# First image behind attention: constants in three packed loads, later expert weights, half a norm beside half a net, tap sums through GpSimd

## Chip, core and metric

The kernel runs on one core of a Trainium2 chip. The metric is the device time of one execution in microseconds (us). A profile shows one execution on that core; its times count from the first instruction of that execution. The engines are called PE (TensorE; PEld are its weight loads), DVE (VectorE), ACT (ScalarE), POOL (GpSimd) and SP (SyncE, which here only issues loads and stores). ACT and POOL issue loads as well; the profile writes ACTq and SPq for that part of an engine.

## What is computed

Four images of 384 channels and 32 x 32 pixels go through two layers, all in fp32:

```python
# layer 0
x = x + attention(ln_c(x))      # 8 heads, relative tables for q, k and v, then out @ w_proj + b_proj
t = tokens(x)
t = t + ffn(ln_t(t))            # weights are kron products: 384 -> 1536 (gelu) -> 384
# layer 1
x = x + conv(ln_c(x))           # depthwise: 7x7 + 5x3 + 3x5 + (1x7 then 7x1) + (1x5 then 5x1) + biases
t = tokens(x)
t = t + moe(ln_t(t))            # 4 experts, 2 per token, 384 -> 1536 (gelu) -> 384, weighed by the gates
```

ln_c and ln_t both normalise one pixel over its 384 channels.

## The kernel before, in words

The work goes in three phases. qkv_phase computes queries, keys and values and writes them to DRAM. attention_phase runs over the eight heads, and within a head over the 32 image rows; its order is written out by hand and pinned. rest_phase does everything else, image by image. Within rest_phase a scheduler orders what isn't pinned, by the dependences of the operations, and the generators that are stepped side by side decide what it may mix.

Channels lie on the 128 partitions in three chunks (KC = 3), pixels along the free side. An image of 1024 pixels is worked in two halves of 512 (TOK).

**End of attention** (L628 to L637). The last head's second half of rows is finished behind the loop: the values are multiplied (values), the reciprocal sums go to DRAM (keep, rd), four table products are added to the result o (value_table, add_table), and for each of the two groups of images a spread of the reciprocals is loaded (spread, tile rb, one buffer) and multiplied into o on POOL (normalise, L490). The result is stored to ao_d by two transfers that POOL issues (store, L494). The first half of the rows was stored before, by SP.

**Constants** (const, L906). 24 arrays are loaded into a tile each, by 24 transfers on ACT's queue. w_proj and b_proj belong to the projection, fold, c_fc and c_proj to the net, w77 to b35 to the convolution, gate_w to slot0 to the gates and to the lists of slots. A transfer has one of eight completion counters, given out in turn to the transfers of SP and ACT together; one that is given a counter waits until the transfer that had it before has landed.

**Image 0, front** (front, L926). For each half the attention's result (tile at) and x (into xb) are loaded by SP; then both halves are projected (L948), added to x (L951) and their statistics taken (token_stats, L65: PE transposes a block of 128 pixels into row_ps, DVE takes mean and variance); then the net runs over one half after the other (L958 to L1000): u_ps is the folded input, f_ps the hidden layer, which ACT turns by Gelu into hs, o_ps gathers it, and ffn_ps spreads it back to the channels, to be added to xb (L997). fold is scaled and centred before (L1375 to L1377); its sum_ps matmuls stand in PE's line between the first matmul of the projection and the others.

**Behind front.** preload(wts[0]) (L1380) loads two blocks of expert weights of 2.5 MB each by SP. POOL clears img, the padded image (L1381). combined (conv_weights, L705) adds the small convolutions into the 7 x 7 weights, on DVE.

**Image 0, convolution** (first, L1326). normalise (L1004) takes statistics of both halves, and writes (x - mean) to xc and the factors to scale_sb; image (L1018) multiplies them into img. Then the 49 taps are shared: DVE does channel chunk 0 and four rows of chunk 1 by multiply-adds (convolve, L1038), PE does the rest in four parts (taps_by_matmul, L1058): for each part 98 matmuls with diagonal weights (made by POOL, L1064, two products of 3136 elements each) into two banks, which ACT copies (L1092); two matmuls add the copies into a third bank (taps_ps, a single buffer, L1093), and DVE adds that to xb (L1096). gates (L1129) need the whole of xb; gate_ps (L647) is their first matmul.

**After that** the front, norm and convolution of images 1 to 3 run beside the experts' blocks (blocks, L1189 on; e_ps and y_ps are theirs), with a planner that steps a list of others() by costs (more, L1402).

Of the kernel before, what the change touches and what calls it, by code (L numbers as in the profile page):

```python
# [11 lines left out]
F32 = mybir.dt.float32  # L12
AF = mybir.ActivationFunctionType
ALU = mybir.AluOpType
# [4 lines left out]
P = 128  # L19
B, C, IMG = 4, 384, 32  # L20
N = IMG * IMG
# [22 lines left out]
HS = 5  # L44
# [8 lines left out]
NOT_LAST = (2 * (B - 1) * N + NEXP * (BLK - 1)) // BLK - sum(COUNTS[:-1])  # L53
MAXB = B * N // BLK
OUTSIDE = 1e6


def bcast(ap, dim, n):
# [133 lines left out]
def attention_phase(tc, cst, held, tabs, tv, qk_d, v_d, ao_d, heads):  # L192
# [31 lines left out]
    with ExitStack() as es:  # L224
# [252 lines left out]
            dst = o.rearrange("p g (y x) -> p g y x", x=IMG)[: 64 + HD, :, :, XT * g : XT * (g + 1)]  # L477
            nc.gpsimd.tensor_tensor(dst, dst, tvs, ALU.add)

        def spread(rd, g):  # L480
            rb = work.tile([P, YT * IMG], F32, tag="rb", name="rb", bufs=1)
            for r in range(2):
                dma(
                    rb[64 * r : 64 * r + 64],
                    bass.AP(rd.tensor, rd.offset + (2 * g + r) * N, [[0, 64], [1, YT * IMG]]),
                )
            return rb

        def normalise(o, g, rb):
            nc.gpsimd.tensor_tensor(o[:, g], o[:, g], rb, ALU.mult)  # L490

        def store(h, o, y, issue=dma):
            for r in range(2):
# [29 lines left out]
        for n, h in enumerate(heads):  # L523
# [104 lines left out]
            if not last:  # L628
                batch = (h, o, IMG - 1, keep(rT))
                blk = nblk  # L630
        values(o, IMG - 1)
        rd = keep(rT)
        for g in range(IMG // XT):
            add_table(o, g, value_table(g))
        for g in range(2):
            normalise(o, g, spread(rd, g))
        store(heads[-1], o, IMG - 1, nc.gpsimd.dma_start)  # L637


def gate_logits(nc, pools, ident, gw, x, logits):  # L640
# [64 lines left out]
def conv_weights(nc, const, pool):  # L705

    w7, bias = const("w77", [P, KC, 7, 7]), const("b77", [P, KC])
    small = [(const(name, [P, KC, kh, kw]), kh, kw) for name, kh, kw in (("w53", 5, 3), ("w35", 3, 5))]
    lines = [(const(f"w{n}w", [P, KC, 1, n]), const(f"w{n}h", [P, KC, n, 1]), n) for n in (7, 5)]
    biases = [const(name, [P, KC]) for name in ("b53", "b35")]  # L710
    yield w7, bias
    for t, kh, kw in small:
        y, x = (7 - kh) // 2, (7 - kw) // 2
        for k in range(KC):
            dst = w7[:, k, y : y + kh, x : x + kw]
            nc.vector.tensor_tensor(dst, dst, t[:, k], ALU.add)
    for tw, th, n in lines:
        full = pool.tile([P, KC, n, n], F32, name=f"cw_f{n}")
        o = (7 - n) // 2
        for k in range(KC):  # L720
            nc.vector.tensor_tensor(full[:, k], bcast(tw[:, k], 1, n), bcast(th[:, k], 2, n), ALU.mult)
            dst = w7[:, k, o : o + n, o : o + n]
            nc.vector.tensor_tensor(dst, dst, full[:, k], ALU.add)
    for t in biases:
        nc.vector.tensor_tensor(bias, bias, t, ALU.add)


def slot_positions(nc, pools, cst, image, count, total):
# [151 lines left out]
def rest_phase(tc, cst, x, ao_d, ins, xs_d, y_d, x2_d, out):  # L880
# [9 lines left out]
    with ExitStack() as es:  # L890
# [8 lines left out]
        ps_y = es.enter_context(tc.tile_pool(name="r_ps_y", bufs=1, space=PSUM))  # L899
        stp = (small, ps_h, "h")  # L900

        def after(ins_, other):
            sync = mybir.DependencyInfo(mybir.DependencyClass.Sync, mybir.DependencyReason.DATA)
            tc.add_manual_dep(ins_.ins, other.ins.name, sync, reason="slots are written in pieces")

        def const(name, shape):  # L906
            t = wp.tile(shape, F32, name=f"c_{name}")
            nc.scalar.dma_start(t, ins[name])
            return t

        wproj = const("w_proj", [P, KC, C])
# [11 lines left out]
        pc["one"], pc["slot0"] = one, const("slot0", [P, NEXP])  # L923
        img = wp.tile([P, KC, IMG + 6, IMG + 6], F32, name="img")

        def front(b, xb):  # L926

            banks = [(ps_h, "h", None)] * 3 + ([(ps_y, "y", 2)] * 2 + [(ps_y, "t", None)] if b <= 1 else [])  # L930
            halves = [xb[:, :, half * TOK : (half + 1) * TOK] for half in range(2)]
            ats = []
            for half, xs in enumerate(halves):
                at = work.tile([P, KC, TOK], F32, tag="xc", name="at")
                nc.sync.dma_start(at, ao_d[half][:, b].rearrange("(k p) n -> p k n", p=P))
                nc.sync.dma_start(
                    xs, x[b, :, half * TOK : (half + 1) * TOK].rearrange("(k p) n -> p k n", p=P)
                )
                ats.append(at)
                yield 0.0, 0.0  # L940
            for _ in range(3):
                yield 0.0, 0.0
            scales = []
            for at, xs in zip(ats, halves):
                for m in range(KC):
                    ps = ps_h.tile([P, TOK], F32, tag="h", name="proj_ps")
                    for k in range(KC):
                        nc.tensor.matmul(  # L948
                            ps, wproj[:, k, m * P : (m + 1) * P], at[:, k, :], start=(k == 0), stop=(k == KC - 1)
                        )  # L950
                    nc.vector.scalar_tensor_tensor(  # L951
                        xs[:, m, :], ps, bproj[:, m : m + 1], xs[:, m, :], ALU.add, ALU.add
                    )
                    yield 0.7, 2.7

                _, rstd = yield from token_stats(nc, stp, ident, xs, cst["eps5"])
                scales.append(rstd)
            for rstd, xs in zip(scales, halves):  # L958
                scale = to_partitions(nc, (small, ps_m, "m"), ident, one, rstd)
                scale_sb = work.tile([P, TOK], F32, tag="scale", name="scale")  # L960
                nc.scalar.copy(scale_sb, scale)


                ps = ps_m.tile([P, TOK], F32, tag="m", name="u_ps")
                for k in range(KC):
                    nc.tensor.matmul(ps, fold[:, k, :], xs[:, k, :], start=(k == 0), stop=(k == KC - 1))
                u = small.tile([P, TOK], F32, tag="u", name="u")
                nc.vector.tensor_tensor(u, ps, scale_sb, ALU.mult)
                yield 1.4, 3.5

                po = ps_m.tile([P, TOK], F32, tag="m", name="o32_ps")
                pend = []
                for f0 in range(0, NF + 3, 3):
                    phs = []
                    for f in range(f0, min(f0 + 3, NF)):
                        pool, tag, bufs = banks[f % len(banks)]
                        ph = pool.tile([P, TOK], F32, tag=tag, name="f_ps", **({"bufs": bufs} if bufs else {}))
                        lo = f % 4 * 32
                        nc.tensor.matmul(ph, c1t[lo : lo + 32, f // 4, :], u[lo : lo + 32, :], start=True, stop=True)
                        phs.append((f, ph))  # L980
                    for f, hs in pend:
                        lo = f % 4 * 32
                        nc.tensor.matmul(
                            po[lo : lo + 32, :], cp1t[:, f, :], hs, start=(f < 4), stop=(f >= NF - 4)
                        )
                    pend = []
                    for f, ph in phs:
                        hs = hid.tile([P, TOK], F32, tag="hs", name="hs", bufs=HS)
                        nc.scalar.activation(hs, ph, AF.Gelu)  # L989
                        pend.append((f, hs))  # L990
                    yield 0.0, 2.2
                o32 = small.tile([P, TOK], F32, tag="u", name="o32")
                nc.scalar.copy(o32, po)
                for m in range(KC):
                    ps = ps_h.tile([P, TOK], F32, tag="h", name="ffn_ps")
                    nc.tensor.matmul(ps, spread[:, m * P : (m + 1) * P], o32, start=True, stop=True)
                    nc.vector.scalar_tensor_tensor(  # L997
                        xs[:, m, :], ps, cp2[:, m : m + 1], xs[:, m, :], ALU.mult, ALU.add
                    )
                yield 2.1, 2.7  # L1000

        pause = wp.tile([P, 1], F32, name="pause")

        def normalise(xb, halves):  # L1004

            for half in range(2):
                xs = xb[:, :, half * TOK : (half + 1) * TOK]
                mean, rstd = yield from token_stats(nc, stp, ident, xs, cst["eps6"])
                mps = to_partitions(nc, (small, ps_m, "m"), ident, one, mean)
# [39 lines left out]

        wts = [[wp.tile([P, WROW], F32, name=f"w{i}{fh}") for fh in range(2)] for i in range(2)]  # L1050

        def preload(w):
            for fh in range(2):
                nc.sync.dma_start(w[fh], ins["w12"][fh * P : (fh + 1) * P, :])

        none = wp.tile([P, 2, 1], F32, name="none")
        nc.vector.memset(none, 0.0)
        def taps_by_matmul(xb, parts):  # L1058
# [15 lines left out]
            for k, y0, ny in parts:  # L1074
# [18 lines left out]
                    nc.tensor.matmul(po[64 * h : 64 * h + 64, :n], half, e[:, :n], start=True, stop=True)  # L1093
                yield
                acc = xb[:, k, y0 * IMG : y0 * IMG + n]
                nc.vector.tensor_tensor(acc, acc, po[:, :n], ALU.add)  # L1096
                yield

        def new(shape, name, dt=F32):
# [223 lines left out]
            yield from gates(b)  # L1323
            yield from scatter(b, pause)

        def first():  # L1326


            half, own = IMG // 2, 4
# [2 lines left out]
                xbs[0], [(2, 0, half), (2, half, half), (1, own, rest), (1, own + rest, rest)]  # L1332
            )
            next(taps)
            halves = []
            yield from normalise(xbs[0], halves)
            yield from image(halves)
            for _ in convolve(0, xbs[0], [(0, 0, IMG), (1, 0, own)]):
                for _ in range(3):
# [35 lines left out]
        for k in range(KC):  # L1375
            nc.vector.tensor_scalar_mul(fold[:, k, :], fold[:, k, :], cf2[:, k : k + 1])
        center(nc, ps_m, "m", one, fold)  # L1377
        for _ in enter(0):
            pass
        preload(wts[0])  # L1380
        nc.gpsimd.memset(img, 0.0)  # L1381
        for _ in combined:
            pass
        center(nc, ps_m, "m", one, gw)
        reached = set()
        todo = others()
        for i, _ in enumerate(first()):
            if 6 <= i < 8:
                next(todo)
        for i, _ in enumerate(dispatch(0)):  # L1390
# [128 lines left out]
```

## Time and profile before

| what | value |
|---|---|
| median of 9 runs | 3103.27 us |
| lowest, highest | 3094.65, 3106.81 us |
| the profiled execution's own time | 3101.2 us |
| its span, first to last instruction | 3099.4 us |
| mean granted clock of PE | 0.976 |
| busy over the span: PE, DVE, ACT, POOL | 2927.0, 1928.6, 1378.7, 1165.6 us |
| last product of attention on PE ends | 1500.1 us |
| convolution of image 0 on DVE starts | 1603.4 us |
| gate_ps of image 0 starts | 1701.0 us |

How to read it. A line of a timeline has the start, the busy time, the engine, the line of the kernel, the operation, output<-input, shape, how many, and in brackets how long the engine sat idle before it and what ended that. A line of the waits has who waited for whom, the us in total, the times, and the longest. A line of the chain has the start, the duration and the step; the chain is followed back from the last instruction of the execution to what released each step. Idle time of an engine that nothing waits for costs nothing.

### The profile page before, as it was taken

The page shows a single profiled execution, that of the slowest core. Times are in us where ns is not written, and L with a number is a line of the kernel's source. Part 1 is how long each engine was busy: PE and PEld are TensorE (multiplying, and loading weights), DVE is VectorE, ACT ScalarE, POOL GpSimd, SP SyncE. Part 2 cuts the span into 40 slices and gives each one's busy share as a digit, 9 for nine tenths or more (in the row PEclk, how much of TensorE's full clock was granted, in tenths as well). Part 3 has the DMA queues.
Part 4 walks back from the last instruction along what each step waited for, and adds up shares of the span by engine and source line. Part 5 has one row for each costly group of instructions (what it writes and reads, how often), then busy time and mean ns, then how long its engine had stood idle before and what let it go on. Part 6 is the DMA issues. An engine that isn't in the chain of part 4 may idle for free.

```text
span 3099.4 us, 63826 instructions
## 1 busy us (share of the span) xinstructions
PE 2927.0 (94%) x25591; PEld 2031.5 (66%) x25591; DVE 1928.6 (62%) x3595; ACT 1378.7 (44%) x2839; POOL 1165.6 (38%) x1115
## 2 busy tenths in 40 slices
PE   8997999999999999999698989998999999999996
PEld 4544676767777777677433455664677777778775
DVE  2226787878787878787466699998999610001101
ACT  1105666666666666666220513333342423333332
POOL 3224737474747473737200321131234322114422
PEclk9998999999999999999899999999999999999998
DMA  3796566656565656564401331530444144375852
GB/s 126 261 317 207 134 199 138 200 139 199 139 199 139 199 139 199 134 203 117 164 21 57 126 124 75 219 146 16 171 174 179 41 175 176 143 288 197 310 193 73
DMA packets 265720, 500.56 MB, mean 162 GB/s; under 512 B 137248, under 2 KB 190112, under 8 KB 257744
## 3 DMA queue, kind: packets, MB, share of 16 engines
q1 hardware_dynamic: 168944, 246.73, 25.7%
q0 software_dynamic: 43552, 228.24, 19.9%
q10 hardware_dynamic: 52928, 21.53, 3.6%
q8 instruction: 201, 3.29, 0.5%
q14 instruction: 95, 0.78, 0.1%
HBM read 543.58 MB, written 152.37 MB: 225 GB/s over the span
## 4 chain that ended last, share of the span: by engine, by line
PE 69%; DVE 12%; issue 10%; DMA 3%; POOL 3%; ACT 2%; ACTq 0%; SPq 0%; POOLq 0%; DVEq 0%
PE e_ps L1243 15%; PE y_ps L1221 14%; PE t_ps L397 8%; DVE xb L1038 7%; PE av_ps L214 7%; PE sc_ps L214 7%; PE tabq_ps L214 5%; PE a_ps L407 3%; PE tv_ps L214 2%; PE tabk_ps L214 2%; DVE extra L389 1%; DVE oT L466 1%; PE row_ps L74 1%; PE qk_ps L162 1%; DMA qk_d<-qk_sb 1%
## 5 line engine op out<-in xcount | busy, mean ns | idle before, releaser
L1243 PEld LDWEIGHTS e_ps<-xT,w 128*128 128x128 f32 x4824 | 654.7, 193 | 229.7 <-ACT hs L989 16.1
L340 POOL TENSOR_TENSOR bias<-b,s 128x416 f32<-128x416 f32 (+24 forms) x656 | 659.6, 1044 | 171.5 <-DMA s<-sd 155.1
L1243 PE MATMUL e_ps<-xT,w 128*128 128x128 f32 x4824 | 673.2, 277 | 19.7 <-DVE xb L951 8.0
L1221 PE MATMUL y_ps<-w,eh 128*128 128x384 f32 x1608 | 650.9, 489 | 6.1 <-ACT eh L1246 6.1
L1246 ACT ACTIVATE eh<-e_ps,w 128x128 f32<-128x128 f32 x804 | 294.1, 368 | 740.3 <-PE e_ps L1243 728.8
L1038 DVE SCALAR_TENSOR_TENSOR xb<-img,c_w,xb 128x1024 f32<-128x1024 f32 (+1 forms) x539 | 611.3, 1199 | 0.0
L1211 POOL DMA_INDIRECT w<-in_w,row x134 | 163.1, 1217 | 773.0 <-PE y_ps L1221 265.7
L389 DVE TENSOR_REDUCE extra<-arow 128x32 f32<-128x32 f32 (+24 forms) x768 | 381.3, 555 | 9.9 <-ACT arow L378 5.8
L368 DVE CUSTOM_DVE_ANT_0 arow<-sc_ps,bias 128x1024 f32<-128x1024 f32 x256 | 312.6, 1221 | 95.4 <-issue 52.6
L397 PEld LDWEIGHTS t_ps<-ident,arow 128*128 128x128 f32 x2048 | 220.5, 142 | 173.0 <-ACT aT L398 100.6
L378 ACT ACTIVATE arow<-arow,nm 128x1024 f32<-128x1024 f32 x256 | 302.9, 1183 | 65.0 <-DVE nm L368 64.9
L398 ACT COPY aT<-t_ps 128x512 f32<-128x512 f32 x512 | 278.9, 604 | 93.2 <-PE t_ps L397 92.9
L1224 DVE TENSOR_TENSOR yo<-y_ps,w 128x384 f32<-128x384 f32 x67 | 37.3, 557 | 443.4 <-PE y_ps L1221 443.4
L397 PE MATMUL t_ps<-ident,arow 128*128 128x128 f32 x2048 | 282.3, 281 | 15.1 <-ACT arow L378 15.1
L214 PE MATMUL sc_ps<-kk,qs 48*32 48x512 f32 x4096 | 277.5, 605 | 6.3 <-DVE nm L368 5.4
L1221 PEld LDWEIGHTS y_ps<-w,eh 128*128 128x128 f32 x1608 | 247.9, 193 | 18.5 <-ACT eh L1246 7.7
L214 PEld LDWEIGHTS av_ps<-aT,vb 128*64 128x64 f32 x4096 | 222.3, 137 | 51.3 <-ACT aT L398 40.4
L214 PE MATMUL av_ps<-aT,vb 128*64 128x128 f32 x4096 | 237.7, 274 | 0.0
L305 DVE STREAM_TRANSPOSE b<-tabk_ps 128x480 f32<-128x480 f32 x256 | 218.3, 981 | 23.4 <-PE tabk_ps L214 22.4
L214 PE MATMUL tabk_ps<-tab,kq 48*128 48x480 f32 x512 | 222.9, 582 | 6.0 <-DVE b L305 6.0
L214 PE MATMUL tabq_ps<-tab,kq 48*128 48x480 f32 x512 | 219.9, 578 | 2.2 <-ACT aT L398 1.5
L309 ACT COPY st<-tabq_ps 128x480 f32<-128x480 f32 x256 | 142.6, 561 | 70.1 <-PE tabk_ps L214 41.8
(215 smaller groups left out, 3190.5 us busy)
## 6 DMA issues: line engine op xcount, KB each, us to landing
sd<-st SPq DMA_DIRECT2D x128, 480.0 KB, 2.5
s<-sd SPq DMA_DIRECT2D x256, 240.0 KB, 3.6
xs_d<-zero POOLq DMA_DIRECT2D x8, 3072.0 KB, 13.9
tvw<-in_tv SPq DMA_DIRECT2D x120, 192.0 KB, 4.1
y_d<-yo SPq DMA_DIRECT2D x67, 192.0 KB, 1.9
qk_d<-qk_sb POOLq DMA_DIRECT2D x48, 256.0 KB, 7.4
qs<-qk_d SPq DMA_DIRECT2D x256, 48.0 KB, 2.8
kq<-qk_d ACTq DMA_DIRECT2D x56, 192.0 KB, 3.8
```

What stands on the lines that cost most here:

```text
L214: ins = nc.tensor.matmul(*args, **kw)
L305: turn = nc.vector.transpose(b2.rearrange("p e y x -> p x (e y)")[:, i + j], ps[:, j, : SPAN * IMG])
L340: nc.gpsimd.tensor_tensor(bias[:, y0:y1, :], bass.AP(b2.tensor, b2.offset + (e * IMG + y0) * IMG, [list(b2.ap[0]), [(step * IMG + 1) * IMG ...
L368: nc.vector.tensor_tensor_reduce(s["flat"], ps.rearrange("p h n -> p (h n)"), s["bias"].rearrange("p y x -> p (y x)"), -SCALE, BIG, ALU.ad ...
L378: nc.scalar.activation(s["flat"], s["flat"], AF.Exp, bias=s["nm"], scale=-1.0, accum_out=dn[:, y % YT : y % YT + 1])
L389: pin(nc.vector.tensor_reduce(ex[:, i, :], a[:, p0:p1, :].rearrange("p y x -> p x y"), AX.X, ALU.add))
L397: pin(nc.tensor.transpose(pt[:, j, :], s["flat"][:, k0 : k0 + P], ident))
L398: pin(nc.scalar.copy(aT[:, 4 * g : 4 * g + 4, s["y"] % YB, :], pt))
L1038: nc.vector.scalar_tensor_tensor(acc[:, k, y0:y1], img[:, k, dy + y0 : dy + y1, dx : dx + IMG], w7[:, k, dy, dx : dx + 1], acc[:, k, y0:y1 ...
L1221: nc.tensor.matmul(py, hs, w[:, o : o + C], start=(ff == 0), stop=(ff == NF - 1))
L1243: nc.tensor.matmul(ph, w[:, o : o + P], xT[k][:, c, :], start=(c == 0), stop=(c == KC - 1))
L1246: nc.scalar.activation(hs, ph, AF.Gelu, bias=w[:, o : o + 1])
```

## The change

Five things, all between the end of attention and the gates of image 0:

1. The 24 constants are packed on the host into three arrays (PACKS): w_proj with b_proj; the net's; the convolution's, the gates' and the lists'. Three pinned transfers on ACT's queue bring them, and const hands out views.
2. At the end of attention both spreads are loaded ahead of the last values, the second into a buffer of another tag; one normalise runs on DVE, the other on POOL; SP issues the stores instead of POOL.
3. For image 0 SP's order is pinned: at and x of half 0, x and at of half 1, then the two blocks of expert weights.
4. front is cut into loads, project and net. For image 0, normalise of half 0 is stepped beside the net of half 1 and followed by the normalise of half 1. Clearing img, conv_weights and the centring of gate_w are recorded behind that.
5. conv_weights runs on POOL. The sum of a tap part is copied by ACT from taps_ps and added to xb by POOL.

```diff
+PACKS = [
+    (("w_proj", KC * C), ("b_proj", KC)),
+    (("c_fc_2", KC), ("fold", KC * P), ("c_fc_1", NF // 4 * P), ("c_proj_1", NF * 32), ("c_proj_2", KC), ("spread", C)),
+    (
+        ("w77", 49 * KC), ("b77", KC), ("w53", 15 * KC), ("w35", 15 * KC), ("w7w", 7 * KC), ("w7h", 7 * KC),
+        ("w5w", 5 * KC), ("w5h", 5 * KC), ("b53", KC), ("b35", KC), ("gate_w", KC * 32), ("gate_b", NEXP),
+        ("before", P), ("blocks", MAXB), ("wrow", 2), ("slot0", NEXP),
+    ),
+]
...
-        def normalise(o, g, rb):
-            nc.gpsimd.tensor_tensor(o[:, g], o[:, g], rb, ALU.mult)
+        def normalise(o, g, rb, engine=nc.gpsimd):
+            engine.tensor_tensor(o[:, g], o[:, g], rb, ALU.mult)
...
+        rd = keep(rT)
+        rbs = [spread(rd, 0), spread(rd, 1, "bias", 3)]
         values(o, IMG - 1)
-        rd = keep(rT)
         for g in range(IMG // XT):
             add_table(o, g, value_table(g))
-        for g in range(2):
-            normalise(o, g, spread(rd, g))
-        store(heads[-1], o, IMG - 1, nc.gpsimd.dma_start)
+        normalise(o, 0, rbs[0], nc.vector)
+        normalise(o, 1, rbs[1])
+        store(heads[-1], o, IMG - 1)
...
         def const(name, shape):
-            t = wp.tile(shape, F32, name=f"c_{name}")
-            nc.scalar.dma_start(t, ins[name])
+            pack, at = PLACES[name]
+            if pack not in packs:
+                packs[pack] = wp.tile([P, WIDTHS[pack]], F32, name=f"pack{pack}")
+                pin(nc.scalar.dma_start(packs[pack], ins[f"pack{pack}"]))
+            n = int(np.prod(shape[1:]))
+            t = packs[pack][:, at : at + n]
...
+                pair = [
+                    (at, ao_d[half][:, b].rearrange("(k p) n -> p k n", p=P)),
+                    (xs, x[b, :, half * TOK : (half + 1) * TOK].rearrange("(k p) n -> p k n", p=P)),
+                ]
+                for dst, src in pair[::-1] if half and not b else pair:
+                    ins_ = nc.sync.dma_start(dst, src)
+                    if not b:
+                        pin(ins_)
...
-                nc.vector.tensor_tensor(acc, acc, po[:, :n], ALU.add)
+                e = hid.tile([P, TOK], F32, tag="hs", name="taps", bufs=HS)
+                nc.scalar.copy(e[:, :n], po[:, :n])
+                nc.gpsimd.tensor_tensor(acc, acc, e[:, :n], ALU.add)
...
-        for _ in enter(0):
-            pass
-        preload(wts[0])
+        xbs[0] = xp_.tile([P, KC, N], F32, name="xb", tag="xb")
+        xs0, xs1 = halves_of(xbs[0])
+        halves = []
+        at0, at1 = result(loads(0, xbs[0]))
+        preload(wts[0], pin)
+        rstd0 = result(project(xs0, at0))
+        rstd1 = result(project(xs1, at1))
+        result(net(0, xs0, rstd0))
+        side = normalise(xbs[0], halves, (0,))
+        for _ in net(0, xs1, rstd1):
+            next(side, None)
+        result(side)
+        result(normalise(xbs[0], halves, (1,)))
         nc.gpsimd.memset(img, 0.0)
         for _ in combined:
             pass
```

In conv_weights every nc.vector becomes nc.gpsimd. The generator first no longer normalises; it is given the halves. For images 1 to 3, front calls loads, project and net in the old order.

## The prediction, made before the changed kernel ran

> **What bounds the kernel now.** The page's share by engine (PE 94%) is an average over stages; the change touches only the stretch between the end of attention and the first experts, so I read that stretch: busy time by stages first, then who waited for whom there, then the chain that ended last, then the timeline around the taps. First the stages (columns: stretch; length; busy us and count on PE, PEld, DVE, ACT, POOL; granted clock; DMA share; GB/s):
>
> ```profile
> 1500.00:1539.00 39.00, 15.28 (x42) 7.83 (x38) 12.31 (x48) 0.00 (x0) 18.18 (x7) 0.68 0.89 309
> 1539.00:1567.00 28.00, 26.92 (x95) 10.26 (x95) 9.39 (x22) 11.11 (x19) 0.00 (x0) 0.96 0.02 5
> 1567.00:1581.00 14.00, 13.16 (x61) 4.11 (x59) 1.52 (x3) 6.81 (x14) 0.00 (x0) 1.00 0.00 0
> 1581.00:1604.00 23.00, 19.13 (x70) 7.00 (x72) 19.56 (x36) 3.02 (x5) 0.00 (x0) 0.78 0.12 39
> 1650.00:1699.00 49.00, 41.16 (x392) 18.60 (x384) 26.80 (x38) 0.97 (x2) 0.00 (x0) 0.90 0.10 41
> ```
>
> For 39 us after attention no engine is half busy and the DMA engines are at 89%: image 0 waits for loads. Which ones, the waits and the chain say:
>
> ```profile
> SPq L935 <- DMA c_b<-in_b: 10.6, 1, 10.6
> DVE b_slot L820 <- DMA c_slot<-in_slot: 8.8, 1, 8.8
> DVE cw_f L721 <- DMA c_w5h<-in_w5h: 6.3, 1, 6.3
> PE row_ps L74 <- DVE s_st L76: 9.7, 3, 9.3
> ```
>
> ```profile
> 1525.63 10.61 DMA c_slot<-in_slot
> 1536.27 1.28 DVE b_slot L820
> 1537.55 0.49 DVE s_st L76
> 1538.08 0.90 PE row_ps L74 x3
> 1538.98 9.00 PE proj_ps L948 x18
> ```
>
> The reader is to see that a constant of 2 KB (slot0), the last of 24 loads on ACT's queue, landed 10.6 us after its issue, beside the 5 MB of expert weights; that a small VectorE operation for a list needed much later stood in line for it; and that the norm's statistics, the banks and the second half's projection stood behind that one. Attention's second half (SP, L935) could not even be fetched before 1525.1. The taps' stall is in the timeline:
>
> ```profile
> 1665.73 2.79 PE L1082 MATMUL tap_ps<-img,w 64*64 64x448 f32 x24
> 1668.61 0.97 ACT L1092 COPY taps<-tap_ps 128x448 f32<-128x448 f32 x2 [20.45 <-PE tap_ps L1082]
> 1675.47 0.70 DVE L1096 TENSOR_TENSOR xb<-xb,taps_ps 128x512 f32<-128x512 f32 x1
> 1676.32 1.76 PE L1093 MATMUL taps_ps<-taps,half 128*64 128x448 f32 x4 [7.80 <-DVE xb L1096]
> 1678.01 20.95 PE L1082 MATMUL tap_ps<-img,w 64*64 64x448 f32 x196
> ```
>
> The one bank of taps_ps was read by VectorE, behind 98 multiply-adds of the convolution (done at 1675.6), so PE waited 7.8 us and went on at a lower clock.
>
> **Part 1, loads (packs, expert weights later, attention's last store).** The instruction lists of both builds differ only from 1490 to 1705; before and behind that the order on every engine is the same. ACT issues 3 loads instead of 24 (0.4 us each, so until about 1501.7 instead of 1526). At 1503 to 1524 the DMA engines moved 278 to 428 GB/s, mean 327. Ahead of pack 1's end stand at and xb of the first half (0.79 MB each), pack 0 (0.59) and pack 1 (0.79): 2.95 MB, of which 0.37 are moved by 1503, so pack 1 lands at 1503 + 2.58/0.327 = 1510.9. The fold (three VectorE products, six sum matmuls in PE's line ahead of 16 of the first half's 18 projection matmuls) waits for it; before, c_fold let it start at 1509.6 and the projection ended at 1519.8, 10.2 later. So the first projection ends at 1521.1. Image 1 shows the same step with nothing in the way: its first half's projection ends at 1716.6, the second's starts at 1719.2, 2.65 later. So the second projection starts at 1523.8 instead of 1539.0: **-15.2**. Next late is attention's second half. Its two rb loads now go out at 1490 to 1492.6; one norm goes to VectorE (0.7), the other stays on GpSimd behind the 3.7 us memset of img (1504.1 + 1.26), so the stores go out on SP at 1505.4, behind 3.25 MB in both queues: moved by 1511.8, their 0.39 by 1513, landed by about 1514. at for half 1 is issued then, behind xb of half 1 (2.4 us of data); it took 4.6 from issue to landing before, at of half 0 took 6.4: landed 1519 to 1523. That is 1 to 5 us ahead of need. Bounds of this part: pack 1 at 1509.6 (as c_fold) to 1514, and at as late as 1528: -17 to -10. The weights (two loads, 5 MB, about 14 us at this rate) now follow at; the first experts run after 1760, so their delay is hidden by over 200 us.
>
> From the second projection to the next f_ps image 0 took 14.8 us (1539.0 to 1553.8), partly at clock 0.5 to 0.6; image 1 at full clock 14.0 (1719.2 to 1733.2): **-0.9** (0 to -1).
>
> The 20 tap sums go from VectorE to GpSimd (GpSimd's 32-element rows took 0.26 us): 5 to 6 us from pack 2's landing at about 1512, then two diagonal products of 5.4 us: first done at about 1524, needed at 1570. Free, by 46 us of cover.
>
> What speaks against GpSimd here is in two rows. b_slot took 1.28 us at 1536.27 and 0.15 to 0.16 in three other places; it ended when GpSimd's diagonals (1526.68, 10.84 us) ended. And the 4-element begin (L831) took 2.18 us, until GpSimd's memset ended. The Trainium skill, "SBUF — State Buffer", section "Who interferes with whom", has the rule: VectorE with two SBUF inputs and a GpSimd operation that reads SBUF exclude each other for a whole instruction. It would add nothing by my order, and one diagonal more if b_slot lost its place.
> By the rows alone: b_slot now comes some 5.5 us behind pack 1, at 1516.4, the first diagonal at 1518. If the diagonal wins, b_slot, and the first half's xb behind it, stand until 1523.4 (xb was due at 1522): +2, or +7 for both diagonals. I take 0 and keep +7. The four adds of the taps (1.26 each) lie beside VectorE's multiply-adds: at most 5 us more there, and VectorE ends 14 us ahead of PE (below).
>
> **Part 2, norm of half 0 beside the net of half 1.** Before, from the second u_ps to o_ps' end 13.35 us (1566.98 to 1580.33), PE busy throughout. Now 12 transposes (0.27 each), two all_ps (1.0 each) and two table loads (1.28 each) with a root and a scale copy go in between. I walked through the new order with those durations: u at +3.5 us, statistics until +7.2, root at +8.8, second all_ps at +10.8, ACT back at Gelu at +11.8, last o_ps at +17.9: **+4.5** (2 to 8). Then only one half's norm is left. Before, the step from the last xb (1584.6) to the taps' steady run was 15.1 us (1599.69, with 97 of 98 tap matmuls of the part left). Now the same row's times give means' product at 1587.5, xc 1589.3, second all_ps done 1593.0, three gate sums 0.8: 1593.8, with 14 taps already done in the gaps, half 0's image being there. 5.9 us of start and 13 taps of 0.22: **-8.7** (-7 to -9).
>
> **Part 3, taps' sums over ACT and GpSimd.** Part 3 to part 4: from the end of taps at 1668.5 to their start at 1678.0, 9.5 us; part 2 to 3, without the stall, 2.2: -7.3. Part 4 then ran 20.95 against 19.30 for part 3: -1.6. Together **-8.9** (-7 to -9). At the end of part 4 the chain gets an ACT copy (0.54) and a GpSimd add (1.14 for 448 elements) in place of VectorE's 0.62, ahead of gate_ps: **+1.1** (0.9 to 2). VectorE, whose convolution would start at about 1585 and take 71.7 us, ends at 1656, PE's taps at 1671: PE stays the bound.
>
> **Sum:** -15.2 - 0.9 + 4.5 - 8.7 - 8.9 + 1.1 = -28.1. All that follows keeps its order and hangs on gate_ps, so I carry it through whole. The profiled execution took 3101.2 us (span 3099.4), the median of the nine runs is 3103.3: 3073.1 and **3075 us** as a median.
>
> **Rivals.** (a) *The gap is given back inside.* at lands late or a diagonal holds VectorE (+7), the mixed net costs +8 instead of +4.5, a tap start is lost: speaks for it that the first projection already waits on the same DMA engines at 89%; against it that at of half 1 landed in 4.6 us with 2.5 MB issued right behind it. About 3075 + 11 = 3086.
> (b) *Bandwidth is the bound anyway.* The packs carry the same 1.7 MB; if at shared the engines evenly with the 5 MB behind it, it would land at 1514 + 5.9/0.39 (381 to 394 GB/s at 1527 to 1539) = 1529 and the second projection start there: +5, 3080. Against it: c_slot was on the other queue, at on the weights' own.
> (c) *Nothing gained behind gate_ps:* the chain's later waits take it up, 3103. Against it: the 774 us of GpSimd idle and the DMA loads there follow PE's blocks; I find no wait of that size that does not hang on image 0.
> (d) *Slower: GpSimd's small sums.* Taps and the bias add now wait for 20 GpSimd operations on strided slices of pack 2. They decide from (1570 - 5.4 - 1512)/20 = 2.6 us each; at 4.4 us the taps come 35 us late and the kernel ends near 3110. The nearest row is 0.26 us, ten times less.
>
> **How the numbers follow.** Forecast 0.60 (3066 to 3082), (a) 0.17, (b) 0.11, a larger gain 0.03, (c) 0.04, (d) 0.05. The bounds' best, -33, is 3070, their worst, near -12, 3091; with 2 to 3 us for medians the range is 3066 to 3091. Within 0.2% (6 us, about what a measurement of this kernel can tell from no change) 0.04, slower 0.05, faster 0.91.
>
> **What would show it.** Right: second projection at about 1524 (from the span's start), no wait on a constant in VectorE's list but pack 1's, u_ps of half 1 to o_ps' end 18 us, taps running before the last xc, gaps between tap parts of 2 to 3 us each, gate_ps near 1673. Wrong: a second projection that waits for at, b_slot over 1 us with PE behind it, o_ps beyond 22 us, or gate_ps earlier by 28 with the end not following.

## The result and the profile after

The changed kernel takes 3089.03 us (median of 10 runs, 3083.26 to 3092.8) against 3102.97 us (31 runs of the kernel before): ratio 0.9953, 95% interval [0.9945, 0.9962]. It is 14 us faster; the forecast was 28 us, and the range 3066 to 3091 holds the time near its upper end. The profiled execution took 3092.86 us (span 3090.9).

The spans of the two profiles differ by 8.5 us only, mainly because attention, which the change leaves alone until its last lines, ended at 1508.3 in this execution and at 1500.1 in that of before. Over all 14 profiles of this case it ended between 1499.9 and 1508.9. So every mark below is counted from attention's last product on TensorE. gate_ps, on which everything later hangs, starts 200.8 us behind it before and 181.7 after: -19.1 where -28.1 was forecast. From gate_ps to the end it is 1398.4 and 1400.9.

The stages of the changed kernel (columns as in the prediction: stretch; length; busy us and count on PE, PEld, DVE, ACT, POOL; granted clock; DMA share; GB/s):

```profile
1508.00:1531.00 23.00, 13.78 (x50) 7.29 (x45) 8.96 (x30) 0.00 (x0) 15.54 (x24) 0.78 0.92 343
1531.00:1558.00 27.00, 25.92 (x95) 10.04 (x95) 10.21 (x23) 11.12 (x19) 4.22 (x1) 1.00 0.37 150
1558.00:1576.00 18.00, 17.47 (x70) 5.73 (x68) 8.86 (x15) 9.77 (x16) 0.00 (x0) 1.00 0.13 44
1576.00:1591.00 15.00, 13.86 (x62) 5.22 (x64) 9.84 (x18) 2.75 (x4) 0.00 (x0) 1.00 0.00 1
1655.00:1690.00 35.00, 24.22 (x206) 9.78 (x204) 9.53 (x13) 2.56 (x5) 12.99 (x3) 0.85 0.04 10
```

The 39 us of loads are 23 us now, at about the same share of the DMA engines (0.92 against 0.89). The net of half 1 (third row) is 18.7 us long, from its first u_ps to the end of o_ps, instead of 13.4, and keeps TensorE busy. The last row is the surprise: in 35 us TensorE is busy for 24, and GpSimd, which did nothing in that place before, is busy for 13. The waits of this stretch, first around the loads, then around the taps (engine, what waits, for what: us in total, times, longest):

```profile
DVE xb L980 <- PE proj_ps L977: 9.5, 6, 2.4
PE proj_ps L977 <- DMA at<-ao_d: 8.6, 1, 8.6
...
POOL pack L730 <- DMA pack<-in_pack: 5.3, 1, 5.3
DVE pack L1423 <- DMA pack<-in_pack: 4.7, 1, 4.7
```

```profile
PE taps_ps L1140 <- ACT taps L1139: 12.3, 5, 9.4
ACT taps L1139 <- POOL xb L1145: 9.9, 1, 9.9
```

No load of a small constant is waited for any more: VectorE's list waits for pack 1 alone. But the taps' stall is still there. Before, TensorE waited 7.8 us for VectorE; now it waits 9.4 for ScalarE, and ScalarE 9.9 for GpSimd. Why GpSimd was late is in the timeline (start, length, engine, line) and in the tile's own rows (durations in ns, min/median/max):

```profile
1592.98 71.55 DVE L1085 SCALAR_TENSOR_TENSOR xb<-img,pack,xb 128x128 f32<-128x128 f32 x98
1612.42 54.45 POOL L1145 TENSOR_TENSOR xb<-xb,taps 128x512 f32<-128x512 f32 x2 [77.20 <-ACT taps L1144]
```

```profile
L1145 POOL TENSOR_TENSOR xb<-xb,taps x4: 1127/1192/53226, 1612.4 to 1690.8; 128x512 f32<-128x512 f32 x2, 128x448 f32<-128x448 f32 x2
```

An add that takes 1.1 to 1.3 us otherwise took 53.2. It ended at 1665.65, 1.1 us after VectorE's train of 98 multiply-adds (1664.53): one usual duration. The add held its buffer of the tag hs (five of them) all that time, so ScalarE had none for part 3's second copy. (The chain below gives that copy's wait; e1 tests that it is the buffer.) The chain that ended last goes through it:

```profile
1612.42 53.24 POOL xb L1145
1665.66 0.02 issue
1665.68 0.54 ACT taps L1139
1666.22 0.04 issue
1666.26 1.76 PE taps_ps L1140 x2
1668.02 20.08 PE tap_ps L1129 x179
```

### The profile page after: what moved, and what is told of

The parts are those of the page before. It is cut to its first block, busy times and chain, and to the rows that moved or that the text cites. A ratio compares the mean times of both kernels' runs of the same rounds, so it can differ in the third digit from the quotient of the medians.

```text
span 3090.9 us, 63805 instructions
## 1 busy us (share of the span) xinstructions
PE 2930.7 (95%) x25591; PEld 2034.4 (66%) x25591; DVE 1924.6 (62%) x3572; ACT 1382.6 (45%) x2845; POOL 1223.8 (40%) x1136
## 4 chain that ended last, share of the span: by engine, by line
PE 71%; issue 11%; DVE 9%; POOL 5%; DMA 3%; ACT 2%; SPq 0%; POOLq 0%; ACTq 0%; DVEq 0%
PE e_ps L1292 15%; PE y_ps L1270 15%; PE t_ps L410 8%; PE sc_ps L227 7%; PE av_ps L227 7%; PE tabq_ps L227 5%; DVE xb L1085 5%; PE a_ps L420 3%; PE tv_ps L227 2%; POOL xb L1145 2%; PE qk_ps L175 1%; PE tabk_ps L227 1%; POOL bias L353 1%; DVE oT L479 1%; PE row_ps L87 1%
## 5 line engine op out<-in xcount | busy, mean ns | idle before, releaser
L1085 DVE SCALAR_TENSOR_TENSOR xb<-img,pack,xb 128x1024 f32<-128x1024 f32 (+1 forms) x539 | 610.8, 1195 | 0.0
L318 DVE STREAM_TRANSPOSE b<-tabk_ps 128x480 f32<-128x480 f32 x256 | 218.6, 981 | 24.3 <-PE tabk_ps L227 22.2
```

What stands on the lines that cost most here:

```text
L318: turn = nc.vector.transpose(b2.rearrange("p e y x -> p x (e y)")[:, i + j], ps[:, j, : SPAN * IMG])
L1085: nc.vector.scalar_tensor_tensor(acc[:, k, y0:y1], img[:, k, dy + y0 : dy + y1, dx : dx + IMG], w7[:, k, dy, dx : dx + 1], acc[:, k, y0:y1 ...
```

## The experiments

Theory after the result: GpSimd's add cannot get at SBUF while VectorE's two-input operations follow one another without a gap, and the buffer that it holds carries the wait to ScalarE and TensorE. Rivals: the wait has another reason (banks, a semaphore); or the forecast's gain went elsewhere. e1 to e4 ran on one chip (the kernel before takes 3101.05 us there), e5 to e8 on a second and e9 to e12 on a third, where the kernel before takes 1% longer (3134.24 and 3134.49); so ratios to before are compared. Differences of ratios are given in us of 3101, in brackets what the two intervals leave open. Marks from one profile each, in us: start of the second projection, end of the taps' part 1 (the first taps_ps) and start of gate_ps, all counted from attention's last product; the pause of TensorE's tap products between parts 3 and 4; gate_ps to the end.

| kernel | ratio [95%] | 2nd proj. | part 1 | pause 3-4 | gate_ps | to end |
|---|---|---|---|---|---|---|
| before | 1 | 38.6 | 123.1 | 9.5 | 200.8 | 1398.4 |
| after | 0.9953 [0.9945, 0.9962] | 22.4 | 101.8 | 12.8 | 181.7 | 1400.9 |
| e1 own place | 0.9931 [0.9918, 0.9945] | 21.8 | 101.2 | 2.0 | 169.5 | 1399.0 |
| e2 sums on VectorE | 0.9953 [0.9939, 0.9967] | 21.5 | 100.9 | 12.4 | 180.3 | 1399.8 |
| e3 gaps in train | 0.9921 [0.9907, 0.9934] | 21.4 | 100.8 | 2.0 | 169.1 | 1400.2 |
| e4 nets, then norms | 0.9970 [0.9960, 0.9979] | 22.0 | 108.8 | 9.4 | 186.6 | 1400.7 |
| e5 one input | one run | 22.2 | 101.6 | 12.1 | 181.2 | 1433.5 |
| e6 24 loads | 1.0013 [0.9999, 1.0026] | 38.9 | 120.1 | 12.8 | 199.8 | 1434.6 |
| e7 weights first | 1.0010 [0.9997, 1.0022] | 36.0 | 120.3 | 12.8 | 201.3 | 1437.5 |
| e8 gaps, 8 rows | 0.9916 [0.9899, 0.9933] | 21.6 | 101.0 | 1.8 | 165.2 | 1438.4 |
| e9 clear | one run | 21.5 | 100.9 | 2.0 | 169.2 | 1430.5 |
| e10 old tail | 0.9973 [0.9959, 0.9988] | 24.7 | 105.6 | 12.8 | 186.9 | 1431.2 |
| e11 sums alone | 0.9975 [0.9964, 0.9985] | 33.2 | 117.5 | 2.0 | 186.1 | 1426.6 |
| e12 small sums | 0.9956 [0.9942, 0.9971] | 21.7 | 101.1 | 12.8 | 182.5 | 1429.4 |

**e1, own place for the copied sums.**

```
-                e = hid.tile([P, TOK], F32, tag="hs", name="taps", bufs=HS)
+                e = wts[1][i // 2][:, 49 * 64 + i % 2 * TOK :]
                 nc.scalar.copy(e[:, :n], po[:, :n])
```

> The copy of a part's tap sums, that GpSimd adds to xb, gets a place of its own (the unused tails of the two weight tiles that hold the diagonals) in place of one of the five hs buffers; nothing else moves. Theory: in the changed kernel GpSimd's first add (53.2 us, the others 1.1 to 1.2) is shut out until VectorE's train of multiply-adds ends, and the hs buffer that it holds carries that to ScalarE (9.9 us) and TensorE (9.4 us) between parts 3 and 4. Then here the first add still takes some 50 us, but TensorE's gap between parts 3 and 4 is 2 to 3 us, from part 1's end to gate_ps 71 us in place of 80.7, and the time 3080 (9 below the changed kernel's 3089). Rival 1: the stall sits in TensorE's banks or in ScalarE's own order: gap still 9 us, time 3089. Rival 2: the stall goes, but what follows gate_ps gives it back: gate_ps 9 us earlier and the time 3087 to 3089.

Measured 3078.21 us, ratio 0.9931. The pause fell from 12.8 to 2.0 us, and gate_ps came 12.2 earlier, 2 to 3 more than expected. By the ratios the kernel is 7 us faster than the changed one (2 to 12). GpSimd was as late as ever (its first three adds lie in one row that ends at 1661.3, VectorE's train at 1657.8):

```profile
1586.28 71.55 DVE L1085 SCALAR_TENSOR_TENSOR xb<-img,pack,xb 128x128 f32<-128x128 f32 x98
1605.72 55.57 POOL L1145 TENSOR_TENSOR xb<-xb,w 128x512 f32<-128x512 f32 x3 [77.18 <-ACT w L1144]
```

So the late add costs next to nothing by itself; the buffer that it holds is what cost TensorE its time. The first rival falls. The second falls too, since the time went down with gate_ps; whether all 12.2 us reach the end, these intervals can't say.

**e2, sums on VectorE as before.**

```
-                e = hid.tile([P, TOK], F32, tag="hs", name="taps", bufs=HS)
-                nc.scalar.copy(e[:, :n], po[:, :n])
-                nc.gpsimd.tensor_tensor(acc, acc, e[:, :n], ALU.add)
+                nc.vector.tensor_tensor(acc, acc, po[:, :n], ALU.add)
```

> The changed kernel with the taps' sums as they were before: VectorE adds them straight from the bank, no copy and no GpSimd add. Theory: the move to GpSimd removed nothing, it only moved the wait from VectorE's line to GpSimd's: VectorE's first add stands behind the train of multiply-adds until about 1664.5, TensorE waits 8 to 10 us after part 3, and the chain to gate_ps loses about 1 us of copy and add at the end: 3086 to 3090, the changed kernel's time within 2. Rival: the forecast's own term was right and something else ate 8.9 us: then this kernel is slower than the changed one by 8.9 less 1.1, 3097.

Measured 3084.77 us, ratio 0.9953, the changed kernel's own. The pause is 12.4 us and TensorE waits 10.7 for VectorE's add:

```profile
PE taps_ps L1140 <- DVE xb L1143: 10.7, 1, 10.7
```

The move of the sums, as the change makes it, is worth nothing: the wait changed its name.

**e3, gaps in the train.**

```
-                    if b:
+                    if True:
                         tc.keep_in_program_order(nc.vector.memset(pause, 0.0))
```

> The changed kernel with one more thing: after each of the 49 steps of image 0's train VectorE clears one element per partition (as it does already for the later images), so that the train has 48 gaps without a two-input read of SBUF. Theory (GpSimd's add is shut out as long as VectorE's two-input operations follow each other without a gap): the four adds get in within some 2 to 3 us each, TensorE's gap between parts 3 and 4 falls from 12.8 to 2 to 3, VectorE's train ends 5 to 10 us later (49 clears of about 0.1, four adds of 1.2) but still ahead of TensorE's part 4: time about 3080. Rival 1 (the add waits for the train's end for another reason, a semaphore or the queue): still some 50 us, time 3089 to 3092. Rival 2 (a gap is too short for it to get in): the same numbers as rival 1, but no wait on a semaphore of VectorE in its row.

Measured 3073.94 us, ratio 0.9921. The adds by tile, and what VectorE did around the first of them (1604.23):

```profile
L1145 POOL TENSOR_TENSOR xb<-xb,taps x4: 1129/1372/2327, 1604.2 to 1671.0; 128x512 f32<-128x512 f32 x2, 128x448 f32<-128x448 f32 x2
```

```profile
1604.16 2.55 DVE L1085 SCALAR_TENSOR_TENSOR xb<-img,pack,xb 128x1024 f32<-128x1024 f32 x2
1605.38 0.06 DVE L1091 MEMSET pause<- 128x1 f32 x1
1606.63 1.55 DVE L1085 SCALAR_TENSOR_TENSOR xb<-img,pack,xb 128x1024 f32<-128x1024 f32 x2
```

The add waited for one multiply-add (1.2 us), got in at the clear, ran its 1.1 us, and VectorE stood for about that long (2.55 instead of 1.55). A clear of one element per partition in each step, 0.06 us, is all that GpSimd needs. This is the change with its fault mended: 10 us less than the changed kernel by the ratios (5 to 15), 27.1 us below the kernel before by the medians of this group, 24 by the ratio (20 to 29), against the forecast's 28.1.

**e4, both nets, then both norms.**

```
-        side = normalise(xbs[0], halves, (0,))
-        for _ in net(0, xs1, rstd1):
-            next(side, None)
-        result(side)
-        result(normalise(xbs[0], halves, (1,)))
+        result(net(0, xs1, rstd1))
+        result(normalise(xbs[0], halves))
```

> The changed kernel without the norm of half 0 beside the net of half 1: both nets first, then both norms, as before. Forecast's terms for this part: the mixed net costs 4.5 (measured 5.3 in the profile), the tail behind it is 8.7 shorter (measured 9.5). Theory: undone, the net takes 13.4 from u_ps to o_ps' end again, the tail 38 us, and all that hangs on it comes 4.2 later: 3093. Rival: the mix moves work without a gain, since the taps that it lets start early stop at the same held buffer, whose end is set by VectorE's train: then VectorE's train starts as late and the time changes by what the train's start changes, 0 to 4: 3089 to 3093, to be told apart by the starts of the train and of part 1.

Measured 3092.32 us, ratio 0.9970: 5 us slower than the changed kernel by the ratios (1 to 9), where the forecast's terms make 4.2. The net took 13.3 us again, but from its end to part 1's end it was 46.5 us (33.7 after, 42.9 before), so part 1 came 7.0 later. (It is longer than before because the centring of gate_w now stands behind the norms: its sum_ps takes TensorE 1.5 us there, and VectorE waits 4.0 us for it.) 3.4 of it were given back where TensorE's pause shrank from 12.8 to 9.4 (VectorE's train ended 6.0 us behind part 3 instead of 9.4), 1.2 lost again in part 4: gate_ps 4.9 later. The theory's number, but the rival has its share in it: the held buffer ate part of what the mixed net gains.

**e5, one input, and e9, a clear, in place of GpSimd's add.**

```
-                nc.gpsimd.tensor_tensor(acc, acc, e[:, :n], ALU.add)
+                nc.gpsimd.tensor_copy(acc, e[:, :n])        e5
+                nc.gpsimd.memset(e[:, :n], 0.0)             e9
```

> The changed kernel with GpSimd copying the taps' sums onto xb in place of adding them (one input from SBUF in place of two; what the convolution and the residual had in those rows is left out of the result, the order of work is the same). Theory as first put (two reads of SBUF shut each other out): a copy with one input is not shut out, each of the four takes about 1 us, TensorE's gap between parts 3 and 4 is 2 us, span as with gaps in the train, some 10 us less than the changed kernel's. Rival: any GpSimd operation that reads SBUF is shut out as long as VectorE's two-input train runs: the first copy takes some 50 us, gap 9 to 12 us, span as in the changed kernel.

> The changed kernel with GpSimd clearing the copied sums' buffer in place of adding it to xb (no read of SBUF at all; the taps' sums are left out of the result; the held hs buffer is the same). The copy with one input was shut out like the add. Theory now (whatever goes between GpSimd and SBUF is shut out while VectorE's two-input train runs): the first clear takes some 50 us, TensorE's gap between parts 3 and 4 is 9 to 12 us. Rival (it is the read that is shut out): all four clears take 0.5 to 1 us, gap 1.3 to 3 us, part 1's end to gate_ps 69 us in place of 80.

One tile row each, first e5, then e9:

```profile
L1145 POOL COPY xb<-taps x4: 563/582/52596, 1607.9 to 1685.9; 128x512 f32<-128x512 f32 x2, 128x448 f32<-128x448 f32 x2
```

```profile
L1145 POOL MEMSET taps<- x4: 472/498/525, 1611.9 to 1678.7; 128x512 f32 x2, 128x448 f32 x2
```

The theory as first put fell with e5: a copy with one input is shut out just like the add (52.6 us, pause 12.1). The theory as widened fell with e9: a clear is not shut out at all (0.5 us, pause 2.0). What stands is the rival of e9: beside the train, GpSimd can write SBUF, and cannot read it. One thing more differs in e9: the clear writes taps, while add and copy write xb, VectorE's own tile. No run has a GpSimd read beside the train that leaves xb alone; but in e10 and e11, below, the two engines hold each other up with no tile in common.

**e6, the packs taken apart, and e7, the weights first.**

```
-            if pack not in packs:
-                packs[pack] = wp.tile([P, WIDTHS[pack]], F32, name=f"pack{pack}")
-                pin(nc.scalar.dma_start(packs[pack], ins[f"pack{pack}"]))
             n = int(np.prod(shape[1:]))
-            t = packs[pack][:, at : at + n]
+            t = wp.tile([P, n], F32, name=f"c_{name}")
+            pin(nc.scalar.dma_start(t, ins[f"pack{pack}"][:, at : at + n]))
```

```
+        preload(wts[0], pin)
         at0, at1 = result(loads(0, xbs[0]))
-        preload(wts[0], pin)
```

> The changed kernel with the packs taken apart again: the same pinned order, the weights still behind attention's loads, but 24 loads of constants on ScalarE's queue. Theory (the small operation b_slot behind the last of 24 loads held VectorE's line; the packs' share of part 1 is most of it): the last load is issued some 25 us after attention's end and lands some 8 us later, the second projection starts 33 to 37 us after attention's last product in place of 22.5, and the time is 3089 + 11 to 14 = 3100 to 3103. Rival: it was the expert weights' place behind attention's loads that paid; the small loads then land right behind their issue and the second projection moves by less than 4: 3089 to 3093.

> The changed kernel with the two loads of expert weights (5 MB) issued ahead of attention's loads on SP again, packs kept. Theory (forecast's part 1: at and the packs stand behind what is ahead of them in the DMA engines): the first projection's at and pack 1 share the engines with 5 MB, 14 us at the rate of before; the second projection starts 8 to 14 us later than in the changed kernel, time 3097 to 3103. Rival: with the packs the loads are so few that the weights' place no longer matters: within 3 us, 3087 to 3092.

Each of them alone gives back the whole change: ratios 1.0013 and 1.0010. In e6 the second projection started 38.9 us after attention, 16.5 later than in the changed kernel, about where it was before; VectorE's wait list and the chain name slot0 again:

```profile
DVE b_slot L834 <- DMA c_slot<-in_pack: 17.9, 1, 17.9
```

```profile
1519.94 17.14 DMA c_slot<-in_pack
1537.08 0.02 issue
1537.10 0.16 DVE b_slot L834
1537.26 0.67 DVE xb L978
```

In e7 the first projection's at is what is late. In SP's pinned order it now stands behind the weights and the stores, so it was issued 7.1 us after attention's last product instead of 0.1, and then it took 16.0 us to land instead of 8.3:

```profile
1510.51 15.95 DMA at<-ao_d
1526.46 0.04 issue
1526.50 8.78 PE proj_ps L977 x14
```

Of the 14.5 us that the first projection starts later than in the changed kernel, the later issue makes 7.0 and the longer way 7.7. The second projection came at 36.0. By the ratios e6 is 19 us slower than the changed kernel and e7 18, 4 to 5 more than the most that was expected. In e7's profile the net of half 1 also took 23.5 us instead of 18.7, at a granted clock of 0.60 from 1577 to 1589; whether that belongs to the edit one profile can't say.

**e8, gaps and eight rows on VectorE.** e3's edit, and:

```
-            half, own = IMG // 2, 4
+            half, own = IMG // 2, 8
```

> Gaps in VectorE's train, and eight rows of channel block 1 on VectorE in place of four, so that the taps' parts 3 and 4 on TensorE have 12 rows each in place of 14. From the profile with gaps: TensorE's last taps_ps at 1669.0, VectorE's train done near 1660. A part of 448 columns takes 20.0 us, one of 512 takes 22.7, so 64 columns less are 2.7 us: 5.4 us for both. VectorE's four more rows are 49 times 4 times 0.0337 us, an estimate from the planner's cost of a row in the code: 6.6 us. TensorE would be done 15 us ahead of that profile's gate_ps less 5.4, VectorE at about 1667, 3.5 us ahead of the old gate_ps: time 3 to 4 below the kernel with gaps alone: 3070. Rival: VectorE becomes the bound with its adds and the lock of GpSimd's adds: 3074 to 3077.

gate_ps started 165.2 us after attention, 3.9 before e3's, as expected. The ratio is 0.9916 [0.9899, 0.9933] against e3's 0.9921 [0.9907, 0.9934]: the two can't be told apart. In e8's profile the stretch from 1704 to 1725, in the next image's net, took 21.2 us where e3 took 3.8, at a granted clock of 0.77; it was not tried whether that recurs. Both beat the kernel before and the changed one.

**e10, attention's old tail.**

```
-        rd = keep(rT)
-        rbs = [spread(rd, 0), spread(rd, 1, "bias", 3)]
         values(o, IMG - 1)
+        rd = keep(rT)
...
-        normalise(o, 0, rbs[0], nc.vector)
-        normalise(o, 1, rbs[1])
-        store(heads[-1], o, IMG - 1)
+        for g in range(2):
+            normalise(o, g, spread(rd, g))
+        store(heads[-1], o, IMG - 1, nc.gpsimd.dma_start)
```

> The changed kernel with the last head's end as before: the two rb loads after the values, both norms on GpSimd, the stores on GpSimd's queue; packs, pinned order and weights as changed. Forecast's part 1 had the second half's at 1 to 5 us ahead of need with the new tail. Worked out from the rows: rb loads some 2 us, GpSimd's memset 3.7 and two norms of 1.26, so stores 9 to 10 us after attention's last product, landed at 12, at landed at 17 to 20, needed at 22.5: the second projection within 0 to 3 us of the changed kernel's, time 3089 to 3092 by the ratio of that chip (0.995 to 0.996). Rival: the old tail is what held at (it was issued 25 us after attention's end): second projection at 30 or later, ratio 0.998.

Measured ratio 0.9973, 6 us slower than the changed kernel (1 to 12), nearer to the rival's number; yet the rival's reason is wrong, for the second projection started at 24.7, not at 30. The rest came by a way that neither had: the second norm stood in GpSimd's line behind the small sums, the diagonals moved back, and the second of them held VectorE's s_dg, which takes 0.69 us elsewhere:

```profile
1515.67 1.26 POOL L503 TENSOR_TENSOR oT<-oT,rb 128x512 f32<-128x512 f32 x1
1522.97 10.84 POOL L1110 TENSOR_TENSOR w<-half,pack 128x3136 f32<-128x3136 f32 x2 [4.57 <-DVE b_step L828]
1528.57 5.79 DVE L115 TENSOR_TENSOR s_dg<-ident,s_rstd 128x512 f32<-128x512 f32 x1
```

**e11, the sums alone.** The kernel before with e3's edit, and the copy and the GpSimd add of the change in place of VectorE's add (the reverse of e2's diff).

> The kernel before with part 3 alone and the gaps in VectorE's train: sums copied by ScalarE and added by GpSimd, one element cleared after each step of image 0's train; loads, norms and all else as before. Theory: this is the forecast's part 3 with its failed step mended: 7.3 to 8.9 gained between the parts, 1.1 lost at the end, no add above 3 us: ratio 0.9975 (7.8 of 3103). Rival: without the earlier start of the taps the sums gain nothing: 1.000.

Measured 0.9975 [0.9964, 0.9985], the ratio that the forecast's part 3 makes (7.8 of 3103; the interval leaves 5 to 11). In the profile part 1's end to gate_ps fell from 77.7 to 68.6, 9.1 us, and no add took over 2.3 us. That the ratio fits to the digit is in part chance: in this profile the second projection started at 33.2, 5.4 earlier than in that of before, with the same loads, because VectorE's b_slot found slot0 landed and was held by the first diagonal only (4.81 us):

```profile
1532.34 10.85 POOL L1064 TENSOR_TENSOR w<-half,c_w 128x3136 f32<-128x3136 f32 x2 [10.65 <-DVE b_first L825]
1532.99 4.81 DVE L820 SCALAR_TENSOR_TENSOR b_slot<-done,c_slot 128x4 f32<-128x4 f32 x1
```

**e12, the small sums on VectorE.**

```
-            nc.gpsimd.tensor_tensor(dst, dst, t[:, k], ALU.add)
+            nc.vector.tensor_tensor(dst, dst, t[:, k], ALU.add)
...
```

> The changed kernel with the 20 small sums of the tap weights back on VectorE. In the program's order they stand between the fold's first products and its last, and wait for pack 2, which landed 10.5 us after attention's last product. GpSimd took 4.0 us for them. Theory: VectorE's line, with the fold and the first xb behind them, ends 3 to 4 us later, the second projection too: ratio 0.996 to 0.997 against 0.9953 for the changed kernel. Rival: the forecast's 0 (the move was free and bought nothing): same as the changed kernel within 0.0005.

Measured 0.9956 [0.9942, 0.9971], second projection at 21.7, no later than in the changed kernel (22.4): the rival. The interval alone would also hold the theory's 0.996 to 0.997; the mark decides. Moving these 20 operations neither paid nor cost, as the forecast said.

## Why the prediction was right, and where it failed

- **Part 1 (-15.2): right in the profiles.** The second projection moved from 38.6 to 22.4, -16.2. Pack 1 was in use 8.7 us after attention's end (10.8 forecast), at of half 1 landed 4.4 us ahead of its use. What the sum did not say is that the pieces don't add: without the packs (e6) or without the weights behind at (e7) nothing is left, without the new tail (e10) it is 6 us less. How much of the 16.2 is the profile's own is open: e11, with the loads of before, had the second projection at 33.2.
- **Second projection to f_ps (-0.9)**: 13.8 against 15.0, -1.2. (The forecast took 14.8 for before, from the chain's 1538.98; the projection's first product started at 1538.77.)
- **Part 2 (+4.5, then -8.7)**: the mixed net +5.4, the tail from the net's end to part 1's end -9.2, together -3.8 against the forecast's -4.2. Until the end of part 1 the stage is 21.3 shorter, 20.3 forecast.
- **Part 3 (-8.9, then +1.1): this step failed.** From part 1's end to gate_ps it is 2.2 us more, not 7.8 less. The failing sentence is "The four adds of the taps (1.26 each) lie beside VectorE's multiply-adds: at most 5 us more there". It took the cost of the two engines' exclusion to be one instruction per add, and to fall on VectorE; and it did not ask which buffer a late add holds. So the term that took away TensorE's wait between parts 3 and 4 (-7.3) was not earned: the pause went from 9.5 to 12.8 us instead of 2.2. The runs showed that the cost falls on GpSimd and lasts as long as the train (53.2 us), that it is GpSimd's read that is shut out (e5, e9), that the held hs buffer brings it to TensorE (e1), and that a gap ends it (e3: 68.3 us from part 1's end to gate_ps, -9.4). The kernel before had the hint in it: from image 1 on, `if b:` puts that clear behind each step of VectorE's train.
- **Luck.** The forecast's own band, 3066 to 3082, does not hold 3089; the whole range does, by an upper end that was drawn for a late at, a diagonal in VectorE's way and a dearer net. None of these made the loss, so that the time lies inside says nothing for part 3.
- **The rest.** 10.0 of the 14 us between forecast and result are this step; e3, where it is mended, has a median of 3073.94. The other 4 can't be put down to one term: gate_ps to the end was 2.5 longer in the profile, and part 1's size is open as said.
- **Rivals.** (a)'s number, 3086, is the nearest, by another way than it gave. (d), the small sums, took 4.0 us in all and cost nothing (e12). (b) did not come: at of half 1 landed in 5.8 us with the weights issued right behind it; a load that shares the engines with the weights is to be seen in e7. (c) did not happen: gate_ps to the end stayed at 1398 to 1401 in the profiles of before, after and e1 to e4.

The Trainium skill, "SBUF — State Buffer", section "Who interferes with whom", was cited for a lock of one whole instruction. The runs agree with it that a GpSimd operation that reads SBUF and a two-input VectorE operation exclude each other, and that one that only writes does not meet this lock (e9). They differ on how long the loser can wait: 53.2 us, through all that was left of the train.

## What to carry to other kernels

Before work moves to an idle engine, ask what it shares with the engine that it leaves, for the longest stretch in which that engine does not pause: a wait there can be as long as the stretch, not as one instruction. Then ask what the late operation holds meanwhile; giving it a buffer of its own (e1) was worth as much to the path as ending its wait (e3). And where several loads stand in one queue of bytes, their orders must be changed together: either half of part 1 was worth nothing alone.

## What the runs showed of the hardware

- Beside a train of 98 back-to-back two-input VectorE operations, of which some 70 were still to come, a GpSimd add took 53.2 us and a copy 52.6 (usual 1.13 to 1.26 and 0.56 to 0.60); a clear took 0.5. A one-element clear on VectorE between two steps lets the add in: 1.1 to 2.3 us.
- It goes the other way too: GpSimd's diagonals (5.4 us each) held a VectorE product for 5.79 us in e10 (usual 0.69), and the 4-element b_slot for 4.81 us in e11 (usual 0.15).
- A GpSimd clear is not free of VectorE in every case: begin, a VectorE operation on 4 elements with one input, ended with GpSimd's 3.71 us clear of img both before (begin 2.18 us long) and after (1.45).
- A load of 2 KB, the last of 24 on its queue, took 17.1 us from issue to landing in e6, while 5 MB of weights were under way on another queue.
- The same kernel took 3101 us on one chip and 3134 us, 1% more, on two others. From gate_ps to the end it is 1398 to 1401 us in the profiles of before, after and e1 to e4, and 1427 to 1438 in those of e5 to e12, so most of the difference seems to lie there; these are different kernels, and there is no profile of the kernel before from the two slower chips.
